# Attention with a mixture of experts on one core: the beginning, the router's order and the passage to the experts, changed together

## The chip, the cores and the metric

The kernel runs on one core of a Trainium2 chip. The metric is the device time of one execution in microseconds (us); several runs give a median, and one more execution is recorded by the hardware profiler. PE is TensorE, DVE is VectorE, ACT is ScalarE, POOL is GpSimd and SP is SyncE, which here only issues DMAs.

## The reference, cut to what matters

The input x has 8 batches of 1024 tokens and 512 features, in float32. The layer is attention with sine and cosine features, then a mixture of 8 experts.

```python
t = arange(S).reshape(1, S, 1, 1); xh = layernorm(x).reshape(B, S, H, dh)       # H 16, dh 32
Q = concat(cos, sin of xh / (1 + |w_q|) + b_q + t * phi_q)      # table of 2048 points
K = concat(cos, sin of xh / (1 + |w_k|) + b_k + t * phi_k)
V = cos + sin of xh / (1 + |w_v|) + b_v
attn = softmax(causal(Q K^T / sqrt(2 * dh))); o = attn V
x = x + cos + sin of o / (1 + |w_out|) + b_out
xn = layernorm(x)
probs = softmax(xn Wr + br); top_p, top_e = top_k(probs, 2)
slot of a token in its expert = its place in order, kept if under 160 for each batch
y = relu(rows W1[e] + b1[e]) W2[e] + b2[e]                      # W1 512x2048, W2 2048x512
x = x + sum over its two experts of top_p * y
```

## The kernel before, in words

All of it is one function. The order of the work on PE, DVE, ACT and SP is the order of the program text; POOL's instructions alone are placed by a scheduler. The text gets its fine order from generators: a piece of work yields at points where other work may be put between, and `some`, `rest` and `with_asides` advance such generators by a step or to their end.

**Beginning** (until the loop). `load_x(0)` (L147) issues eight DMAs of 256 KB on SP for the first batch. ACT's queue issues three row loads (w_v, b_v, b_out, L167), then six for `vec_in`, from which PE and DVE make `vecs`, the columns of constants for q and k. `first_stats` and `layernorm_first` normalise batch 0 on DVE. `make_base(c)` (L443) makes the table t * phi + b for four heads (index c), reduced to one turn: an iota and, for c < 2, the affine step on POOL, the rounding on ACT or DVE, and a 1 MB write to `base_d`, from which later batches read it back. Tables 0 and 1 are made before the loop, 2 and 3 inside of it by `load_base`. Table 1 lies in the buffer of `x_mid` (`room[0]`), as does the scratch for rounding (`room[1]`).

**Attention loop.** It runs over n = 0 to 31, n = 4 b + c: batch b, four heads c. In a step PE makes scores of the heads of n in two pairs (`ps_s`, three buffers of two banks), ACT takes their exponentials (`e`), PE multiplies them with v (`attend`, `av`) and turns the result by token (`turn`). Beside it run, for later steps, `qk_pre` (turning xn, and qk_f by DVE, L508), the sines on ACT, `qk_post` (products on DVE and DMAs into the tiles `qk`), `v_pre` and `v_post`, `layernorm1` of the next batches, and `o_pre`, `o_post` for n - 1, which add the attention's result to `x_mid`.

**Router.** At the first step of a batch (`begin`) the router of the batch before starts: statistics, `rstd`, then four groups of two `rows` (xn on DVE, a DMA to `xn_d`), `features` (PE turns them, DVE copies them to `xT`) and `sums` (logits). Then come the choice of two experts and the places. `scatter` writes for each token its number and gate to a list of slots in DRAM, in 16 indirect DMAs on POOL; `fetch_slots` reads the lists into `meta`. `route_on(slot)` advances the router by a step where the text calls it.

**Passage.** At the last step `experts_begin` opens the experts' buffers, loads the first W1 tiles and runs `gather(0)`: six indirect DMAs on POOL fetch 128 rows of xn each, which PE turns. `experts` runs over 16 chunks (expert e; 768 or 512 of its slots) with layer 1 and layer 2 as seven products in place of eight (`product`; six buffers `ps_p` of one bank). Inside chunk 0 the generator `ending` is advanced once for each product of layer 1: it holds `o_post` and the router of the last batch. `mix_w1` makes sums of weights, on POOL in chunk 0. In `layer2` the results are added to the output by `send`, an accumulating indirect DMA on POOL.

Of the kernel before, what the change touches and what calls it, by code (L numbers as in the profile page):

```python
# [11 lines left out]
F32 = mybir.dt.float32  # L12
# [9 lines left out]
P = 128  # L22
# [51 lines left out]
def preln_attn_moe_kernel(  # L74
# [64 lines left out]
    xnp = to_inputs.pool("xnp", 4, **right)  # L139

# [3 lines left out]
    def token_tiles(dram_rows):  # L144
        return dram_rows.rearrange("(t p) d -> p t d", p=P)

    def load_x(b):  # L147
        halves = []
        for h in range(2):
            xt = xnp.tile([P, 4, D], F32, name="xn")  # L150
            if b == 0:
                for t in range(4):
                    nc.sync.dma_start(xt[:, t, :], token_tiles(x[b])[:, 4 * h + t, :])
            else:
                nc.sync.dma_start(xt, token_tiles(x[b])[:, 4 * h : 4 * h + 4, :])
            halves.append(xt)
        xn_tiles[b] = halves


    load_x(0)  # L160

    rows_in, spare = (
        row2.tile([P, D], F32, name="xn2").rearrange("p (i f) -> p i f", f=P)[:NCH, :n, :]
        for n in (3, 2)
    )
# [56 lines left out]
    first_stats(0, 1)  # L222
# [6 lines left out]
    nc.scalar.dma_start(rows_d.rearrange("i (c f) -> c i f", c=NCH), rows_in)  # L229
# [108 lines left out]
    qkt = to_inputs.pool("qkt", 1, **right)  # L338
# [102 lines left out]
    room = []  # L441

    def make_base(c):  # L443


        if not room:
            t = xmp.tile([P, NTT, D], F32, name="x_mid").rearrange("p (i t) d -> p i (t d)", i=2)
            room.extend(t[:, i, :].rearrange("p (i s) -> p i s", i=2) for i in range(2))
# [3 lines left out]
        nc.gpsimd.iota(  # L452
            p, pattern=[[0, 2], [1, S]], base=0, channel_multiplier=0,
            allow_small_or_imprecise_dtypes=True,
        )
# [28 lines left out]
    def load_base(n):  # L484
        if 1 < n < NCH:
            rest(make_base(n))
            return
# [256 lines left out]
    scatters = []  # L744

    def scatter():
        while scatters:
            b, idx, src = scatters.pop(0)
            nc.gpsimd.indirect_dma_start(  # L749
                out=slot_d[b], out_offset=bass.IndirectOffsetOnAxis(ap=idx, axis=0),  # L750
                in_=src, in_offset=None,
            )

    def router(b):
# [28 lines left out]

        last = b == B - 1

        def features(g):
# [67 lines left out]
        for g in range(NTT // 2):  # L854
            xT = features(g)
            yield
# [91 lines left out]
    def fetch_slots(b):  # L948
# [3 lines left out]
        while s0 < (b + 1) * CAP:  # L952
            s1 = min((s0 // P + 1) * P, (b + 1) * CAP)
            nc.gpsimd.dma_start(
                meta[s0 % P : s0 % P + s1 - s0, :, s0 // P, :],
                rows[s0 - b * CAP : s1 - b * CAP],
            )
# [73 lines left out]
    def gather(i):  # L1031

        e, j0, nh = chunks[i]
        xe = pools["xep"].tile([P, NCH, 2, HALF], F32, name="xe")
        for j in range(2 * nh):
            xg = pools["gp"].tile([P, D], F32, name="xg")
            nc.gpsimd.indirect_dma_start(  # L1037
                out=xg, out_offset=None, in_=xn2_d[i % 2],
                in_offset=bass.IndirectOffsetOnAxis(ap=source[:, e, j0 + j, None], axis=0),
            )  # L1040
            yield None
            dst = xe[:, :, j // nh, j % nh * P : (j % nh + 1) * P]
            if i == 0:
# [6 lines left out]
                )  # L1050
            else:
# [14 lines left out]

    def start(gen, box):
# [6 lines left out]
    def mix_w1(i, q):  # L1074
# [6 lines left out]
        mix = nc.gpsimd.tensor_tensor if i == 0 else TT  # L1081
# [52 lines left out]
    def layer2(i, block, hs, aside):  # L1134
# [29 lines left out]
        def send(r):  # L1164
            nc.gpsimd.indirect_dma_start(  # L1165
# [3 lines left out]
            )  # L1169

# [5 lines left out]
        TT(u2, p1, product(5, 4), ALU.add)  # L1176
        TT(u3, u2, product(6, 5), ALU.add)
        p5 = product(4, 3)
        TT(u2, u2, p5, ALU.add)
        TT(u2, u2, p3, ALU.add)  # L1180
        gated(0, 1, u2)
        send(0)
# [16 lines left out]
    def experts_begin():  # L1199
# [55 lines left out]
    next(base0)  # L1255
    rest_of_loads()
    mask()
    first_stats(1, NTT)
# [6 lines left out]
    next(base1)  # L1265
# [204 lines left out]
```

## Time and profile before

| | |
|---|---|
| Median of three runs | 3331.85 us (3321.11 to 3336.68) |
| Profiled execution | 3330.72 us, its span 3329.0 us |
| PE busy | 3203.4 us, 96% of the span |
| DVE, ACT, POOL busy | 2272.0, 1320.9, 429.5 us |
| PE busy in 0 to 150 us | 91.73 us, granted clock 0.92 |
| PE busy in 150 to 1240 us (attention) | 1061.17 of 1090 us, clock 1.00 |
| PE busy in 1240 to 1480 us (passage) | 216.67 of 240 us, clock 0.94 |
| PE busy in 1480 to 3329 us (experts) | 1833.79 of 1849 us, clock 1.00 |

The page gives the share of the span in which each engine is busy, the span in 40 slices, and the costliest groups of instructions by line. A line is that of kernel.py. A wait is told as "engine, tile, line <- what ended the wait". The timeline shows instructions in order of time: start, duration, engine, line, operation, output and input tiles, and in brackets the idle time before it and its cause. The granted clock is the share of TensorE's full clock that the hardware allowed.

### The profile page before, as it was taken

Reading aid. Unit: us, or ns where it says so; the run is one execution under the profiler, and the core shown is the slowest. Engines: PE = TensorE matmul, PEld = TensorE weight load, DVE = VectorE, ACT = ScalarE, POOL = GpSimd, SP = SyncE. Lnnn points to the kernel's source line nnn. Section 1 sums busy time; section 2 is a strip of 40 time slices with the busy share of each in tenths; the row PEclk is TensorE's granted clock in tenths of the full one; section 3 lists DMA queues with packets and bytes.
Section 4 is the critical chain, followed back from the end, with each engine's and each line's share of the span. In section 5 each row is a group of like instructions: output and inputs, shape, how many; then the busy total and the mean of one; then the engine's idle time right before and its main releaser. Section 6 shows DMA issues by size and latency. Waiting matters only on the chain.

```text
span 3329.0 us, 48774 instructions
## 1 busy us (share of the span) xinstructions
PE 3203.4 (96%) x18942; PEld 2172.0 (65%) x18942; DVE 2272.0 (68%) x4975; ACT 1320.9 (40%) x1617; POOL 429.5 (13%) x397
## 2 busy tenths in 40 slices
PE   3999999999999998899999999999999999999998
PEld 1444444444444444588688688688688688688687
DVE  7887878788787675746746846845845845845854
ACT  5788888878787874201101201201201201201201
POOL 2000202020111103321011011011011011011010
PEclk8999999999999999999999999999999999999999
DMA  4445353545535342422322322322322422322321
GB/s 133 117 121 168 106 165 101 167 134 147 174 106 153 87 143 78 126 39 73 111 38 71 114 42 64 117 39 64 117 45 58 121 42 61 119 46 61 114 39 26
DMA packets 234462, 319.74 MB, mean 96 GB/s; under 512 B 21640, under 2 KB 154488, under 8 KB 222200
## 3 DMA queue, kind: packets, MB, share of 16 engines
q1 hardware_dynamic: 211232, 273.37, 27.8%
q0 software_dynamic: 22912, 43.22, 7.4%
q8 instruction: 150, 2.46, 0.3%
q14 instruction: 80, 0.66, 0.1%
q10 hardware_dynamic: 88, 0.02, 0.0%
HBM read 187.62 MB, written 61.82 MB: 75 GB/s over the span
## 4 chain that ended last, share of the span: by engine, by line
PE 59%; DVE 2%; DMA 1%; issue 0%; ACT 0%; POOL 0%; SPq 0%; POOLq 0%; DVEq 0%; ACTq 0%
PE ps_p L1143 28%; PE ps_p L1098 28%; PE av L701 1%; PE ps_t L1054 1%; PE ps_s L667 1%; DMA out_dram<-y,slots 0%; DMA xg<-xn_d,source 0%; DMA xn_d<-xn 0%; DMA w<-in_L_ffn_W_dram 0%; DVE y L1159 0%; PE ps_s L200 0%; DVE w_t L1009 0%; DVE w L1008 0%; DVE t L1083 0%; DVE u L1185 0%
## 5 line engine op out<-in xcount | busy, mean ns | idle before, releaser
L687 ACT ACTIVATE e<-ps_s 128x1024 f32<-128x1024 f32 (+1 forms) x640 | 567.8, 938 | 212.0 <-PE ps_s L667 130.8
L667 PE MATMUL ps_s<-qk 64*128 64x512 f32 (+3 forms) x3072 | 599.4, 508 | 48.5 <-DVE qk_f L508 20.2
L1143 PE MATMUL ps_p<-w,hid 128*128 128x256 f32 x2560 | 569.6, 380 | 0.0
L1143 PEld LDWEIGHTS ps_p<-w,hid 128*128 128x128 f32 x2560 | 484.6, 190 | 66.3
L701 PE MATMUL av<-e,v 128*64 128x512 f32 (+3 forms) x3072 | 526.6, 492 | 0.0
L1143 PE MATMUL ps_p<-w_t,hid 128*128 128x256 f32 x1920 | 430.3, 379 | 0.6 <-DVE w_t L1009 0.6
L667 PEld LDWEIGHTS ps_s<-qk 64*128 64x128 f32 x3072 | 263.3, 189 | 233.3 <-issue 109.4
L1143 PEld LDWEIGHTS ps_p<-w_t,hid 128*128 128x128 f32 x1920 | 361.8, 190 | 48.7 <-DVE w_t L1009 1.0
L701 PEld LDWEIGHTS av<-e,v 128*64 128x64 f32 x3072 | 201.4, 137 | 285.1 <-issue 269.5
L1098 PE MATMUL ps_p<-xe_s,t 128*128 128x256 f32 (+1 forms) x1024 | 299.3, 435 | 4.3 <-DVE t L1083 3.4
L1098 PE MATMUL ps_p<-xe,w 128*128 128x256 f32 (+1 forms) x1024 | 301.8, 438 | 1.1 <-issue 1.1
L1098 PE MATMUL ps_p<-xe,t 128*128 128x256 f32 (+1 forms) x1024 | 296.8, 433 | 0.0
L749 POOL DMA_INDIRECT slot_d<-token,slot x128 | 161.1, 1259 | 1014.1 <-issue 697.3
L1172 ACT COPY p<-ps_p 128x256 f32<-128x256 f32 x40 | 14.8, 369 | 612.9 <-PE ps_p L1143 612.9
L1098 PEld LDWEIGHTS ps_p<-xe_s,t 128*128 128x128 f32 x1024 | 194.4, 191 | 89.4 <-DVE t L1083 7.9
L1098 PEld LDWEIGHTS ps_p<-xe,w 128*128 128x128 f32 x1024 | 194.8, 192 | 83.9 <-issue 4.9
L1098 PEld LDWEIGHTS ps_p<-xe,t 128*128 128x128 f32 x1024 | 194.4, 190 | 80.9 <-issue 0.4
L1037 POOL DMA_INDIRECT xg<-xn_d,source x80 | 78.1, 976 | 1102.8 <-PE ps_t L1054 1020.9
L1165 POOL DMA_INDIRECT out_dram<-y,slots x80 | 126.3, 1579 | 661.8 <-DVE y L1160 522.4
L1113 ACT ACTIVATE p<-ps_p,b_t 128x256 f32<-128x256 f32 (+1 forms) x128 | 65.4, 511 | 330.7 <-DVE y L1159 169.7
L1117 ACT ACTIVATE hid<-hid 128x256 f32<-128x256 f32 (+1 forms) x128 | 60.1, 470 | 321.7 <-DVE hid L1116 321.7
L1130 ACT ACTIVATE hid<-hid,b_more 128x256 f32<-128x256 f32 (+1 forms) x128 | 71.8, 561 | 271.5 <-DVE hid L1129 271.5
(217 smaller groups left out, 3844.8 us busy)
## 6 DMA issues: line engine op xcount, KB each, us to landing
w<-in_L_ffn_W_dram SPq DMA_DIRECT2D x256, 256.0 KB
w<-in_L_ffn_W_dram SPq DMA_DIRECT2D x64, 512.0 KB
qk<-qk_c SPq DMA_DIRECT2D x124, 256.0 KB
qk<-qk_r SPq DMA_DIRECT2D x124, 256.0 KB
qk_base<-base_d SPq DMA_DIRECT2D x28, 1024.0 KB
xn_d<-xn SPq DMA_DIRECT2D x72, 256.0 KB
x_mid<-in_L_attn_x_dram SPq DMA_DIRECT2D x16, 1024.0 KB
out_dram<-x_mid SPq DMA_DIRECT2D x8, 2048.0 KB
```

What stands on the lines that cost most here:

```text
L667: nc.tensor.matmul(ps[:, a, at : at + w], lhsT=pair[r, 1, kb * P : (kb + 1) * P], rhs=pair[r, 0, q0 : q0 + w], start=at == 0, stop=not own ...
L687: nc.scalar.activation(e, ps[:, :, :n], AF.Exp, scale=UNIT * UNIT / math.sqrt(2 * DH))
L701: nc.tensor.matmul(av[a * 64 : (a + 1) * 64, q0 - 512 * h :], lhsT=vt[:, kb, 2 * pr + a, :], rhs=es[i][:, a, at : at + w], start=kb == 0, ...
L749: nc.gpsimd.indirect_dma_start(out=slot_d[b], out_offset=bass.IndirectOffsetOnAxis(ap=idx, axis=0), in_=src, in_offset=None,)
L1037: nc.gpsimd.indirect_dma_start(out=xg, out_offset=None, in_=xn2_d[i % 2], in_offset=bass.IndirectOffsetOnAxis(ap=source[:, e, j0 + j, None ...
L1054: nc.tensor.transpose(ps[:, c, :], xg[:, c * P : (c + 1) * P], ident)
L1098: nc.tensor.matmul(ps, lhsT=weights[:, k, :], rhs=rows[:, k, :], start=k == 0, stop=k == 1)
L1113: nc.scalar.activation(p1, product(b11, a11), AF.Identity, bias=b1_t[:, e * NHC + q : e * NHC + q + 1])
L1117: nc.scalar.activation(h11, h11, AF.Relu)
L1130: nc.scalar.activation(h12, h12, AF.Relu, bias=more)
L1143: nc.tensor.matmul(ps, lhsT=hs[k][:, part, cols], rhs=ws[k][weight], start=k == 0, stop=k == NHQ - 1,)
L1165: nc.gpsimd.indirect_dma_start(out=out, out_offset=bass.IndirectOffsetOnAxis(ap=meta[:, e, jj[r], 0:1], axis=0), in_=ys[r], in_offset=None ...
```

## The change

At the beginning the six loads of `vec_in` become the first on ACT's queue, and the row loads go to SP behind two tiles of x, spread over 128 partitions. The iotas of tables 0 and 1 come before all that needs `vecs`; two memsets go from POOL to DVE. Table 3 is made inside step 0, in the buffer of table 1, and used there; it is not read back. `layernorm1(1, 1)` is no longer called at step 0 (it was called there and at step 2). `load_mid(0)` goes to the end of step 1.

In the router, `v_post` of the next step and the next two `rows` go behind qk_f at `begin`, with one more yield in a group, and the calls of `route_on` in a batch's second step (c = 1) are placed anew. The scatters of a batch are declared free of each other, and `fetch_slots` waits for all of them.

In the passage the rows of slots for chunk 0 are found two steps before the loop's end, the first two gathers go into `xn2` buffers there, and the next two run ahead. `experts` reuses PSUM tile by tile. The last router has more products between its stages (6 behind "tiles", 5 behind "places"), the last two sums of W1 in chunk 0 are on DVE, one W1 load and `find_rows(1)` and `gather(1)` come earlier, and the sends of chunk 0 are pinned behind the gathers. In `layer2`, for all chunks, the product p5 comes before product(6, 5) and `send(0)` follows it.

```diff
@@ -146,0 +148,6 @@
+    rows_in, spare = (
+        row2.tile([P, D], F32, name="xn2").rearrange("p (i f) -> p i f", f=NCH)[:, :n, :]
+        for n in (3, 2)
+    )
@@ -153,0 +161,8 @@
+                    if (h, t) == (0, 1):
+                        for i, v in enumerate((w_v, b_v)):
+                            nc.sync.dma_start(
+                                rows_in[:, i, :], v.rearrange("h (a f) -> (h a) f", f=NCH)
+                            )
+                        nc.sync.dma_start(
+                            rows_in[:, 2, :], b_out.rearrange("(p f) -> p f", f=NCH)
+                        )
@@ -160,9 +174,0 @@
-    load_x(0)
-
...
-    for i, v in enumerate((w_v, b_v)):
-        nc.scalar.dma_start(rows_in[:, i, :], v.rearrange("(c h) d -> c (h d)", h=HPC))
-    nc.scalar.dma_start(rows_in[:, 2, :], b_out.rearrange("(c f) -> c f", c=NCH))
@@ -173,0 +180 @@
+    load_x(0)
@@ -175,0 +183,8 @@
+    base_first = qkt.tile([P, 2, S], F32, name="qk_base")
+    t = xmp.tile([P, NTT, D], F32, name="x_mid").rearrange("p (i t) d -> p i (t d)", i=2)
+    room = [t[:, i, :].rearrange("p (i s) -> p i s", i=2) for i in range(2)]
+    for t in (base_first, room[0]):
+        nc.gpsimd.iota(
+            t, pattern=[[0, 2], [1, S]], base=0, channel_multiplier=0,
+            allow_small_or_imprecise_dtypes=True,
+        )
@@ -222 +237 @@
-    first_stats(0, 1)
+    first_stats(0, 2)
@@ -229 +244 @@
-    nc.scalar.dma_start(rows_d.rearrange("i (c f) -> c i f", c=NCH), rows_in)
+    nc.scalar.dma_start(rows_d.rearrange("i (p f) -> p i f", f=NCH), rows_in)
@@ -266 +281 @@
-    nc.gpsimd.memset(zero, 0.0)
+    nc.vector.memset(zero, 0.0)
@@ -268 +283 @@
-    nc.gpsimd.memset(empty, 0)
+    nc.vector.memset(empty, 0)
@@ -446,4 +458,3 @@
...
-        p = qkt.tile([P, 2, S], F32, name="qk_base") if c != 1 else room[0]
+        p = (base_first, room[0])[c] if c < 2 else (
+            qkt.tile([P, 2, S], F32, name="qk_base") if c == 2 else room[0]
+        )
@@ -450,0 +462,5 @@
+        if c > 1:
+            nc.gpsimd.iota(
+                p, pattern=[[0, 2], [1, S]], base=0, channel_multiplier=0,
+                allow_small_or_imprecise_dtypes=True,
+            )
@@ -452,4 +467,0 @@
-        nc.gpsimd.iota(
-            p, pattern=[[0, 2], [1, S]], base=0, channel_multiplier=0,
-            allow_small_or_imprecise_dtypes=True,
-        )
@@ -485 +497 @@
-        if 1 < n < NCH:
+        if n == 2:
@@ -486,0 +499 @@
+        if n < NCH:
@@ -744,0 +758 @@
+    scattered = {b: [] for b in range(B)}
@@ -749 +764 @@
-            nc.gpsimd.indirect_dma_start(
+            ins = nc.gpsimd.indirect_dma_start(
@@ -752 +767,4 @@
-            )
+            ).ins
+            for other in scattered[b]:
+                tc.declare_no_dep(ins, other, reason="rows of their own")
+            scattered[b].append(ins)
@@ -765,0 +784,3 @@
+        last = b == B - 1
+        if last:
+            yield
@@ -766,0 +788,2 @@
+        if last:
+            yield
@@ -806,4 +826,0 @@
-            if g + 1 < NTT // 2:
-                ahead[:] = [rows(2 * g + 2), rows(2 * g + 3)]
-                if not last and 2 * g + 4 == NTT:
-                    store()
@@ -811,0 +829,5 @@
+        def next_rows(g):
+            ahead[:] = [rows(2 * g + 2), rows(2 * g + 3)]
+            if not last and 2 * g + 4 == NTT:
+                store()
+
@@ -855,0 +878,4 @@
+            if g + 1 < NTT // 2:
+                if not last:
+                    yield
+                next_rows(g)
@@ -957 +983,9 @@
-            )
+            ).ins
+            for other in scattered[b]:
+                tc.add_manual_dep(
...
@@ -1034,4 +1068,2 @@
-        xe = pools["xep"].tile([P, NCH, 2, HALF], F32, name="xe")
-        for j in range(2 * nh):
-            xg = pools["gp"].tile([P, D], F32, name="xg")
-            nc.gpsimd.indirect_dma_start(
+        def fetch(xg, j):
+            ins = nc.gpsimd.indirect_dma_start(
@@ -1040,0 +1073,11 @@
+            if i in (1, 2):
+                tc.keep_in_program_order(ins)
+            return xg
+
+        def fetch_next(j):
+            return fetch(pools["gp"].tile([P, D], F32, name="xg"), j)
+
+        there = []
+        if i == 0:
+
+            there = [fetch(row2.tile([P, D], F32, name="xn2"), j) for j in range(2)]
@@ -1041,0 +1085,8 @@
+            there += [fetch_next(j) for j in (2, 3)]
+        xe = pools["xep"].tile([P, NCH, 2, HALF], F32, name="xe")
+        for j in range(2 * nh):
+            if len(there) == j:
+                there.append(fetch_next(j))
+            if j or i:
+                yield None
+            xg = there[j]
@@ -1050,0 +1102,2 @@
+                if 1 < j and j + 2 < 2 * nh:
+                    there.append(fetch_next(j + 2))
@@ -1066,0 +1120,5 @@
+    def behind(count, gen):
+        for _ in range(count):
+            yield
+        yield from gen
+
@@ -1081 +1139,2 @@
-        mix = nc.gpsimd.tensor_tensor if i == 0 else TT
+
+        mix = nc.gpsimd.tensor_tensor if i == 0 and q < 6 else TT
@@ -1165 +1224 @@
-            nc.gpsimd.indirect_dma_start(
+            ins = nc.gpsimd.indirect_dma_start(
@@ -1169,0 +1229,2 @@
+            if i == 0:
+                tc.keep_in_program_order(ins)
@@ -1177 +1237,0 @@
-        TT(u3, u2, product(6, 5), ALU.add)
@@ -1179,3 +1239,3 @@
-        TT(u2, u2, p5, ALU.add)
-        TT(u2, u2, p3, ALU.add)
-        gated(0, 1, u2)
+        TT(p1, u2, p5, ALU.add)
+        TT(p1, p1, p3, ALU.add)
+        gated(0, 1, p1)
@@ -1182,0 +1243 @@
+        TT(u3, u2, product(6, 5), ALU.add)
@@ -1203 +1263,0 @@
-        find_rows(0)
@@ -1206 +1266 @@
-        yield from start(gather(0), first_parts)
+        yield from start(first_gather, first_parts)
@@ -1211,2 +1271,2 @@
-        pools["ps_tr"] = to_end.pool("ps_tr", 2, space=PSUM)
-        pools["ps_p"] = to_end.pool("ps_p", 6, space=PSUM)
+        pools["ps_tr"] = to_end.pool("ps_tr", 2, space=PSUM, reuse_waits="tile")
+        pools["ps_p"] = to_end.pool("ps_p", 6, space=PSUM, reuse_waits="tile")
@@ -1219 +1279,2 @@
-                load_ahead(i * NHQ + q + AHEAD)
+                if i or q != NHQ - AHEAD - 1:
+                    load_ahead(i * NHQ + q + AHEAD)
@@ -1230,0 +1292 @@
+                    load_ahead(NHQ - 1)
@@ -1235,0 +1298,2 @@
+            if i == 0:
+                find_rows(1)
@@ -1237,0 +1302,3 @@
+            if i == 0:
+
+                aside = behind(2, aside)
@@ -1239,3 +1306 @@
-                if i == 0 and block == 1:
-                    find_rows(1)
-                layer2(i, block, hs, aside if i or block else iter(()))
+                layer2(i, block, hs, aside)
@@ -1255,0 +1321 @@
+    next(base1)
@@ -1258 +1324 @@
-    first_stats(1, NTT)
+    first_stats(2, NTT)
@@ -1265 +1330,0 @@
-    next(base1)
@@ -1273,0 +1339 @@
+    first_gather = gather(0)
@@ -1280,0 +1347,3 @@
+        if n == NCK - 2:
+            find_rows(0)
+            next(first_gather)
@@ -1295 +1364 @@
-        elif c == 0 and b + 1 < B:
+        elif c == 0 and 0 < b < B - 1:
@@ -1320,0 +1390,3 @@
+            if begin:
+                v_post(n, v_st)
+                next(route)
@@ -1322,0 +1395,2 @@
+            if n == 0:
+                rest(make_base(3))
@@ -1327,2 +1401,2 @@
-        route_on(1)
-        route_on(1)
+        for _ in range(3):
+            route_on(1)
@@ -1339,2 +1412,0 @@
-        if n == 1:
-            load_mid(0)
@@ -1344,0 +1417 @@
+        route_on(1)
@@ -1386,0 +1460 @@
+            route_on(1)
@@ -1391 +1464,0 @@
-        route_on(1)
@@ -1396 +1469 @@
-        if c == 1 and b > 0:
+        if c == 1:
@@ -1400 +1473 @@
-        if more:
+        if more and not begin:
@@ -1427,2 +1500 @@
-        rest(o_post(NCK - 1, o_st))
-        for _ in range(3):
+        for _ in o_post(NCK - 1, o_st):
@@ -1429,0 +1502 @@
+        yield
@@ -1432 +1505 @@
-            for _ in range(5 if name == "tiles" else 1):
+            for _ in range({"tiles": 6, "places": 5}.get(name, 1)):
```

More of the change, by code (lines that the diff above doesn't have):

```diff
@@ L139, in preln_attn_moe_kernel @@
     xnp = to_inputs.pool("xnp", 4, **right)
+    qkt = to_inputs.pool("qkt", 1, **right)
     xn_tiles = {}
@@ L157, in load_x @@
         xn_tiles[b] = halves
-    load_x(0)
-    rows_in, spare = (
-        row2.tile([P, D], F32, name="xn2").rearrange("p (i f) -> p i f", f=P)[:NCH, :n, :]
-        for n in (3, 2)
-    )
-    for i, v in enumerate((w_v, b_v)):
-        nc.scalar.dma_start(rows_in[:, i, :], v.rearrange("(c h) d -> c (h d)", h=HPC))
-    nc.scalar.dma_start(rows_in[:, 2, :], b_out.rearrange("(c f) -> c f", c=NCH))
     vec_in = own.tile([6 * NCH, P], F32, name="vec_in")
@@ L337, in preln_attn_moe_kernel @@
     qkp = to_pairs.pool("qkp", 3, **left)
-    qkt = to_inputs.pool("qkt", 1, **right)
     ps_av = to_pairs.pool("ps_av", 2, space=PSUM)
@@ L439, in preln_attn_moe_kernel @@
     bases = {}
-    room = []
     def make_base(c):
-        if not room:
-            t = xmp.tile([P, NTT, D], F32, name="x_mid").rearrange("p (i t) d -> p i (t d)", i=2)
-            room.extend(t[:, i, :].rearrange("p (i s) -> p i s", i=2) for i in range(2))
-        p = qkt.tile([P, 2, S], F32, name="qk_base") if c != 1 else room[0]
+        p = (base_first, room[0])[c] if c < 2 else (
+            qkt.tile([P, 2, S], F32, name="qk_base") if c == 2 else room[0]
+        )
         r = room[1]
+        if c > 1:
[3 more added lines that the diff above has]
+            )
         affine = nc.gpsimd.tensor_scalar if c < 2 else nc.vector.tensor_scalar
-        nc.gpsimd.iota(
-            p, pattern=[[0, 2], [1, S]], base=0, channel_multiplier=0,
-            allow_small_or_imprecise_dtypes=True,
-        )
         for i in range(2):
@@ L782, in rows @@
             return xn
-        last = b == B - 1
         def features(g):
@@ L953, in fetch_slots @@
             s1 = min((s0 // P + 1) * P, (b + 1) * CAP)
-            nc.gpsimd.dma_start(
+            ins = nc.gpsimd.dma_start(
                 meta[s0 % P : s0 % P + s1 - s0, :, s0 // P, :],
                 rows[s0 - b * CAP : s1 - b * CAP],
-            )
+            ).ins
+            for other in scattered[b]:
+                tc.add_manual_dep(
+                    ins, other.name,
+                    mybir.DependencyInfo(
+                        mybir.DependencyClass.Sync, mybir.DependencyReason.DATA
+                    ),
+                    reason="rows of all scatters",
+                )
             s0 = s1
@@ L1176, in layer2 @@
         TT(u2, p1, product(5, 4), ALU.add)
-        TT(u3, u2, product(6, 5), ALU.add)
-        p5 = product(4, 3)
-        TT(u2, u2, p5, ALU.add)
-        TT(u2, u2, p3, ALU.add)
-        gated(0, 1, u2)
-        send(0)
+        p5 = product(4, 3)
+        TT(p1, u2, p5, ALU.add)
+        TT(p1, p1, p3, ALU.add)
+        gated(0, 1, p1)
+        send(0)
+        TT(u3, u2, product(6, 5), ALU.add)
         TT(ys[1][:, DC:], u3, p5, ALU.add)
```

## The prediction

> **What bounds the kernel now.** The page comes first, for the bound and its holes: its slices, busy tenths of PE and PE's granted clock.
>
> ```profile
> PE   3999999999999998899999999999999999999998
> PEclk8999999999999999999999999999999999999999
> ```
>
> TensorE (PE) is the bound: busy 3203.4 us of the 3329.0 us span. A gain must come from the 126 us in which it is not busy, or from time at a reduced clock. I asked next for PE's waits over the whole span (columns: us in total, times, longest).
>
> ```profile
> PE ps_s L667 <- DVE qk_f L508: 20.2, 7, 7.7
> PE ps_s L200 <- DVE xn L419: 16.4, 1, 16.4
> PE ps_s L667 <- DMA qk<-qk_r: 12.4, 1, 12.4
> PE ps_s L667 <- ACT e L687: 10.3, 7, 5.1
> ...
> PE ps_s L838 <- DVE xT L802: 6.6, 8, 0.8
> PE ps_t L1054 <- DMA xg<-xn_d,source: 4.2, 1, 4.2
> PE ps_s L667 <- DVE xT L802: 3.9, 7, 0.7
> PE ps_t L821 <- DVE prior L904: 3.5, 1, 3.5
> ```
>
> Asked again by stretch, they make four places. **Beginning** (0 to 150 us): 58 us, the 16.4, 12.4 and 10.1 (for vec_in) before the first scores at 42.06 us, then 7.7 for qk_f, 5.3 and 2.9 for exponentials, 2.6 for o_p. **Routers**: 3.1 to 4.6 us in each of seven passes, 23 us in the rows of qk_f (20.2 less 7.7), xT at L838 and xT at L667. **Passage** (1240 to 1480 us, attention to experts): 22.6 us. **Experts**: none from 1500 us on, PE busy 50.00 of 50 us in nearly every stretch, so what changes there in steady state is worth nothing. A few timeline lines carry the rest (start us, us).
>
> ```profile
> 20.74 1.85 DVE L348 TENSOR_SCALAR rstd<-rstd_v 128x8 int32<-128x8 int32 x1
> ...
> 20.70 1.86 POOL L452 IOTA x_mid<- 128x2048 f32 x1
> ...
> 1311.05 4.51 PE L1098 MATMUL ps_p<-xe,w 128*128 128x384 f32 x8 [1.13 <-issue]
> 1315.39 2.74 PE L1098 MATMUL ps_p<-xe_s,t 128*128 128x384 f32 x8
> ...
> 1290.29 0.97 POOL L749 DMA_INDIRECT slot_d<-token,slot  x1 [1.46 <-DMA slot_d<-token,slot]
> ...
> 3321.37 1.55 POOL L1165 DMA_INDIRECT out_dram<-y,slots  x1 [4.03 <-DMA out_dram<-y,slots]
> ```
>
> [...] an 8-column tensor_scalar took 1.85 us beside the iota above, 0.17 us at 244.68 with POOL idle. [...] Eight 384-column matmuls took 4.51 us after the turn into the experts and 2.74 us next; [...] The scatters agree: 0.97 us of POOL, then 1.46 us of waiting for the one before.
>
> **The change part by part.** The sum is made against the profiled execution, 3330.72 us (span 3329.0 and 1.7 around it); that is 1.1 below the median 3331.85 of the runs.
>
> *Beginning, to the first scores.* vec_in's six loads lead ScalarE's queue: three issues less ahead (0.80 to 2.02 us), so 1.2 us earlier. The three row loads go behind two x tiles on SP and are now 128 pieces of 16 bytes each, a form the trace does not show: between no later than now and 3 us late; their DVE chain stands ahead of the copy of vecs, so lateness eats the 1.2. Of the statistics six instead of seven stand behind vecs: -0.8. The two 1.86 us iotas run before vecs is there, and the two memsets moved to DVE cost 0.4. The rstd chain took 5.6 us (20.54 to 26.12), beside an iota and two POOL tensor_scalars; with POOL idle the same chain took 2.3 us (244.47 to 246.7). With small POOL work beside it I take 2.7: -3. The base on ScalarE must be ready too: POOL 4.8 us after vecs, ScalarE 2.3 more, ahead of rstd. Sum -1.2 - 0.8 - 3 + 0.4 = -4.6; bounds -7 and -1. From the first normalised tile (26.20) to the first scores (42.06) nothing changes. SP's zero fills wait a little longer for the memsets, but SP was idle from 23.4 to 30.4: nothing.
>
> *Beginning, n = 0 and 1.* layernorm1(1, 1) at n = 0 goes: it was done again at c = 2. DVE no longer waits 6.8 us for batch one's x, and qk_f comes 8.4 us earlier, so the 7.7 wait goes. But make_base(3) stands next in DVE's order, ahead of t_r. It works in the buffer of base one, so its iota on POOL waits until SP's 1 MB write of that base has landed. That write was issued at 47.48 behind 2 MB of x; DMA was busy until 57.75. Then, in the old clock: landed 58.5, iota 60.4, DVE's 6.3 us (the 100.38 to 106.76 block) 66.7, t_r 67.4, v_p's square 68.5. Behind that square stand the exponentials that PE waits for; they began at 67.25. So +1.2: the 5.1 us wait grows by what the 7.7 us one gave. Bounds: -4 (write landed by 54), +3. At n = 1 DVE loses that 6.3 us block, which made t_r late (110.63) and PE wait 2.92 us; after it 384-column scores ran at 1.98 us for eight against 1.09, so -3.9 with the ramp; bounds -4.5 and -1. make_base(2) and its 2.6 us wait stay. x_mid's 2 MB load moves from mid n = 1 to its end, as in the other batches: nothing, covered by a whole half-pass. **Beginning: -4.6 + 1.2 - 3.9 = -7.3; -15 to +1.**
>
> *Routers, seven passes.* DVE had v (1.22) at 247.68 and xn rows (0.99) at 250.67 ahead of qk_f; both go behind. av_sb must await av until 248.2, so xT starts about 0.5 sooner and qk_f ends 1.3 us sooner than 254.3: of the 1.6 us wait 0.3 stays. xT at L667 goes (0.5). Later in the pass xT goes ahead of qk_f: L838's 0.8 goes, and qk_f ends 1.28 later, where PE has scores and av to do. Sum 2.6 times 7 is 18; I take 14, because qk_r (and ScalarE's squares behind it, which began 1.9 us after it) now waits for 2.2 us of moved work. Bounds: -21, and +8 if that is exposed. The x_n rows' eight DMAs on SP move with them; SP is idle there.
>
> *Passage.* The first two gathers run a pass earlier into xn2, the next two ahead: waits of 2.54 and 2.3 us, and 1.6 of slow matmuls: -5.5, a reserve of 0.9 kept. They stand on POOL ahead of batch 6's scatters (2 us later, needed only in the experts). PSUM reuse by tile at 1311: 1.13 of wait and 1.8 of slow clock; half, -1.5. Router of batch 7 inside chunk 0: 1.7 + 1.9 + 2.4 for xn and xT and 3.4 of slow matmuls; more products lie before the transposes (6 for 5, and DVE's work spread), but xT's copy still has one product to hide in: half, -4.5. "places" gets 5 products, 6.5 us, for 3.5 + 0.7 of waits: -4.2, and 2 of ramp, less 1.2 for what DVE's layer-1 work now stands ahead: -5. The last scatters: 16 at 2.4 us or more, 1378 to 1430; side by side about 1.0 each, so slots, find_rows and gather(1) are ready before PE needs them: 4.2 and about 1 of ramp, -5. Queue order pinned on POOL and the 8 DVE subtractions (some 4 us) that leave POOL: covered by PE at 50 of 50. **Passage: -21.5, taken -20; -30 to -8.**
>
> *Tail.* p5 before product(6, 5) lets send(0) go one product (3.45 us) sooner; send(1) now waits for its landing, 4.03 us. Then DVE's last gating (3318.5) and 0.3 of issue bind, 3318.8 for 3321.15: **-2.3; -3 to -1.**
>
> **Sum:** -7.3 - 14 - 20 - 2.3 = -43.6; 3330.7 - 43.6 = 3287.
>
> **Rivals.**
> A (forecast, 0.70): as above, 3265 to 3306.
> B, waits take the place of waits (0.17): routers give 4, passage 8, beginning 0, tail 2: 3317. For it: in the experts' router DVE and ScalarE alternate within one product, and reordering only moves who is late. Against: 2.4 us of each scatter is waiting, not work, and the tail is a plain chain.
> C, everything gives (0.07): beginning 15, routers 18, passage 28, tail 3: 3267 and below.
> D, slower (0.06): in each router pass the squares of qk_f come late behind v, rows and xT, the next qk is late and PE waits at L667. The other three places give 30, so D decides from 4.3 us a pass on; at 6 it gives 3331 - 30 + 42 = 3343. Against: 1.9 us of slack before the squares, and ScalarE idles 5 us at 282 to 287.
> That the change does not do what it says is a form of B: the scatters would keep 2.4 us of spacing.
>
> **How the numbers follow.** 0.5% (about what a measurement of this kernel can tell from no change) is 17 us, so faster means below 3315: all of A and C and nearly half of B, 0.85; same 0.09, most of B's rest; slower 0.06. The likeliest is A's 3287. The range reaches into B and C: 3264 to 3314.
>
> **What would show it.** First scores near 37 us; PE's 7.7 us wait for qk_f gone but one of 10 us or more for an exponential at n = 0; no wait over 1 us for qk_f in the passes; scatters about 1 us apart; no wait for prior or for xg; POOL's last send 2 us after the last matmul. Wrong if the scatters stay 2.4 us apart, or if PE's waits in 1240 to 1480 us still sum to over 15 us.

## The result, and the profile after

The changed kernel takes 3361.97 us (median; 3357.28 to 3372.11) against 3331.39 us for the kernel before (one run more than in the table above): 1.011 of it, 95% interval 1.0088 to 1.0131. It is slower by 31 us, where 44 us less were forecast. Its profiled execution took 3362.41 us, span 3360.7.

The slices of the page after, PE busy and PE's granted clock in tenths, hardly show where:

```profile
PE   4999999999999998999999999999999999999998
PEclk8999999999999998999999999999999999999999
```

The first slice gained (4 for 3). The next fourteen read 9 as before, because a tenth of an 84 us slice hides 8 us; only the clock's digit falls once, from 9 to 8, in the slice of batch 6's scatters. The totals do show it: the changed kernel's PE is busy for 1040.80 us of 150 to 1240 us, where it was 1061.17. The waits tell more. The profile calls a releaser that it cannot name "remote". The changed kernel has such waits, of ACT and DVE (us in total, times, longest):

```profile
ACT e L700 <- remote: 28.7, 10, 14.5
...
DVE qk_f L521 <- remote: 13.4, 4, 3.4
...
DVE rec L749 <- remote: 10.4, 1, 10.4
```

The kernel before has none. PE's waits over the whole span in the changed kernel (us in total, times, longest):

```profile
PE ps_s L680 <- ACT e L700: 20.6, 9, 9.6
PE ps_s L215 <- DVE xn L433: 13.6, 1, 13.6
PE ps_s L680 <- DMA qk<-qk_r: 12.4, 1, 12.4
PE ps_s L680 <- DVE qk_f L521: 9.1, 9, 4.2
PE ps_s L680 <- issue: 9.0, 6, 2.5
PE ps_s L215 <- issue: 6.3, 5, 1.3
...
PE ps_s L680 <- DVE o_p L751: 5.1, 1, 5.1
PE ps_s L680 <- DVE rec L749: 4.3, 3, 1.6
```

(L680 and L700 after are L667 and L687 before: scores and exponentials.) The row of qk_f has fallen from 20.2, its longest from 7.7, as forecast. New are 15.3 us of waits for "issue", for which the profile shows no releaser (1.1 before), and 9.4 us of waits of L680 for o_p and rec, which had no row before. The scatters of a batch run in bursts of 16. A stretch with such a burst, by engine, first before (columns: PE, PEld, DVE, ACT, POOL busy, PE's clock, DMA share, GB/s):

```profile
500.00:540.00 40.00, 39.95 (x316) 19.37 (x314) 33.95 (x68) 35.96 (x35) 13.49 (x9) 1.00 0.33 80
```

and after:

```profile
500.00:540.00 40.00, 34.29 (x236) 15.62 (x232) 27.99 (x58) 27.07 (x28) 21.69 (x19) 0.91 0.35 80
```

POOL has issued this burst in 23 us in place of 62, and PE, DVE and ACT all lost 6 to 9 us in the same 40. The timeline of the changed kernel in batch 6 shows how:

```profile
1322.98 0.66 PE L215 MATMUL ps_s<-ident,av_sb 64*128 64x64 f32 x16
...
1326.21 2.01 PE L680 MATMUL ps_s<-qk 64*128 64x512 f32 x4 [0.85 <-ACT e L700]
1326.89 0.95 POOL L764 DMA_INDIRECT slot_d<-token,slot  x1 [0.30 <-issue]
1328.15 0.96 POOL L764 DMA_INDIRECT slot_d<-token,slot  x1 [0.30 <-issue]
...
1332.15 0.26 DVE L749 RECIPROCAL rec<-ps_s 128x16 f32<-128x16 f32 x1 [10.43 <-remote]
1332.44 0.69 DVE L751 TENSOR_TENSOR o_p<-ps_s,rec 128x512 f32<-128x512 f32 x1
1333.28 2.08 PE L680 MATMUL ps_s<-qk 64*128 64x512 f32 x4 [5.06 <-DVE o_p L751]
...
1340.18 1.59 POOL L980 DMA_DIRECT2D slots<-slot_d  x2 [2.22 <-DMA slot_d<-token,slot]
1340.66 0.60 ACT L700 ACTIVATE e<-ps_s 128x512 f32<-128x512 f32 x1 [14.51 <-remote]
```

The reciprocal needs only the 16 transposes, which ended at 1323.64. It starts 8.5 us later. ACT stands still for 14.51 us, until the last scatter has landed. From 1328.2 to 1332.1 nothing runs but POOL's scatters, 1.26 us apart (0.96 and 0.30). The work is done; the **signal** that it is done comes late. A signal is here a semaphore event in the trace, on which another engine's wait ends. These can be counted. From a burst's start to 4 us after its last scatter has started, the kernel before has 240 to 256 recorded landing signals of 256 (16 scatters by 16 signals), the changed one 39 to 89. (Even up to the next transfer, which waits for all scatters, the changed kernel has no more than 40 to 95: most landings left no record of their own.) PE's signals come late too. In the kernel before half of them come within 0.02 us of a matmul's end, the latest 0.08 after. In batch 6 of the changed kernel the one for the transposes comes at 1332.12, 8.5 us after their end, and those for two groups of scores, ended at 1325.35 and 1328.22, come at 1340.58 and 1340.64: 15.2 and 12.4 us. That DVE's and ACT's signals are late is not shown: those recorded come within 0.02 us, and after each of PE's waits of over 0.8 us in the bursts PE starts within 0.2 us of the end of a DVE or ACT instruction. But 62 of DVE's 4372 and 27 of ACT's 1473 have no record; in the kernel before it is one, of ACT's.

### The profile page after: what moved, and what is told of

Read it like the earlier page. It is cut to its first block, busy times and chain, and to the rows that moved or that the text cites. A ratio compares the mean times of both kernels' runs of the same rounds, so it can differ in the third digit from the quotient of the medians.

```text
span 3360.7 us, 48765 instructions
## 1 busy us (share of the span) xinstructions
PE 3221.9 (96%) x18942; PEld 2173.8 (65%) x18942; DVE 2252.0 (67%) x4961; ACT 1323.6 (39%) x1617; POOL 417.0 (12%) x387
## 4 chain that ended last, share of the span: by engine, by line
PE 83%; DVE 9%; issue 2%; ACT 2%; DMA 1%; another core or an unknown queue 1%; POOL 0%; SPq 0%; POOLq 0%; DVEq 0%; ACTq 0%
PE ps_p L1202 28%; PE ps_p L1157 25%; PE av L714 14%; PE ps_s L680 12%; ACT e L700 2%; PE ps_s L215 1%; PE ps_s L694 1%; DVE qk_f L521 1%; PE ps_t L1107 1%; DVE qk_r L450 1%; DVE v L450 0%; DVE xT L823 0%; DMA xg<-xn_d,source 0%; ACT hid L1189 0%
## 5 line engine op out<-in xcount | busy, mean ns | idle before, releaser
L700 ACT ACTIVATE e<-ps_s 128x1024 f32<-128x1024 f32 (+1 forms) x640 | 570.2, 938 | 274.4 <-PE ps_s L680 140.7
L680 PE MATMUL ps_s<-qk 64*128 64x512 f32 (+3 forms) x3072 | 612.2, 514 | 66.2 <-ACT e L700 20.6
L714 PE MATMUL av<-e,v 128*64 128x512 f32 (+3 forms) x3072 | 537.2, 500 | 3.5 <-ACT e L700 3.5
L680 PEld LDWEIGHTS ps_s<-qk 64*128 64x128 f32 x3072 | 266.6, 191 | 262.2 <-issue 135.4
L1202 PEld LDWEIGHTS ps_p<-w_t,hid 128*128 128x128 f32 x1920 | 361.9, 190 | 50.4 <-DVE w_t L1043 2.8
```

Source lines behind the costliest of these rows:

```text
L680: nc.tensor.matmul(ps[:, a, at : at + w], lhsT=pair[r, 1, kb * P : (kb + 1) * P], rhs=pair[r, 0, q0 : q0 + w], start=at == 0, stop=not own ...
L700: nc.scalar.activation(e, ps[:, :, :n], AF.Exp, scale=UNIT * UNIT / math.sqrt(2 * DH))
L714: nc.tensor.matmul(av[a * 64 : (a + 1) * 64, q0 - 512 * h :], lhsT=vt[:, kb, 2 * pr + a, :], rhs=es[i][:, a, at : at + w], start=kb == 0, ...
L1202: nc.tensor.matmul(ps, lhsT=hs[k][:, part, cols], rhs=ws[k][weight], start=k == 0, stop=k == NHQ - 1,)
```

## The experiments

Theory **H**: the unchained scatters (none waits for the one before) hold back signals, and the rest of the change gains as forecast. Rival **R**: the router's new order costs the time. Kernels told of together ran on the same chip, beside the kernel before. The chips are called A to F; that of the first comparison is not known. The time in the table is a median; ratios are to the kernel before on that chip. "Last av" is the start of the last matmul of attention with v; "experts" is from there to the end of the last matmul, "tail" from that to the span's end, all from the profiled execution. Each execution here has a recorded span and clock. None was made without recording, so whether recording the signals is part of their load stays untested.

| kernel | chip | time, us | ratio (95%) | last av | experts | tail |
|---|---|---|---|---|---|---|
| before | - | 3331.4 | 1 | 1308.2 | 2009.0 | 11.8 |
| changed | - | 3362.0 | 1.0088-1.0131 | 1354.4 | 1997.1 | 9.2 |
| e1 one by one | A | 3332.3 | 1.0016-1.0041 | 1288.0 | 2030.1 | 9.1 |
| e2 before, side by side | A | 3329.4 | 1.0008-1.0026 | 1308.2 | 2010.5 | 11.7 |
| e3 "spaced" | A | 3301.2 | 0.9919-0.9952 | 1293.6 | 1998.7 | 9.1 |
| e4 "half spaced" | A | 3300.7 | 0.9918-0.9951 | 1293.2 | 1998.5 | 9.2 |
| e5 changed again | B | 3362.6 | 1.0087-1.0131 | 1352.2 | 1999.6 | 9.2 |
| e6 pad alone | B | 3363.0 | 1.0082-1.0129 | 1354.0 | 1996.8 | 9.2 |
| e7 last two side by side | B | 3314.3 | 0.9950-0.9976 | 1302.1 | 1996.3 | 9.2 |
| e8 changed, third | C | 3390.1 | 1.0162-1.0207 | 1392.7 | 1997.7 | 9.2 |
| e9 "spaced" again | C | 3400.3 | 1.0195-1.0234 | 1391.4 | 1998.4 | 9.3 |
| e10 before, side by side | C | 3417.5 | 1.0255-1.0304 | 1393.4 | 2011.3 | 11.7 |
| e11 changed | D | 3391.6 | 1.0155-1.0210 | 1382.0 | 1997.8 | 9.2 |
| e12 wide rows | D | 3375.1 | 1.0111-1.0163 | 1363.1 | 1996.0 | 9.2 |
| e13 four fills between | D | 3326.5 | 0.9979-0.9993 | 1291.0 | 2022.3 | 9.6 |
| e14 two fills between | D | 3313.5 | 0.9932-0.9966 | 1289.3 | 2011.5 | 9.1 |
| e15 fills but last | E | 3302.1 | 0.9919-0.9947 | 1291.2 | 1999.9 | 9.1 |
| e16 chain but last | E | 3305.7 | 0.9930-0.9957 | 1288.3 | 2008.3 | 9.2 |
| e17 gather bursts | E | 3305.5 | 0.9930-0.9960 | 1289.4 | 2005.7 | 8.5 |
| e18 the same again | F | 3303.2 | 0.9919-0.9946 | 1287.6 | 2005.3 | 8.4 |

**Undoing one part, doing it alone (A).** e1 takes the scatters' freedom away, e2 gives it to the kernel before.

```diff
 # e1: scatter() and fetch_slots() as before; e2: these lines added to before
-            for other in scattered[b]:
-                tc.declare_no_dep(ins, other, reason="rows of their own")
```

> The changed kernel with its slot_d scatters waiting for one another again, as before. Theory H (in the changed kernel, 16 scatters 1.26 us apart hold back the signals between the other engines for up to 12 us, some 5 us a batch): the time falls from 3362 by 35 to 60 us, to 3300-3325, below the 3331 of the kernel before; the engines' signals land within 0.1 us again. Rival R (the new order of the router's parts is what costs, and the scatters only show it): the time stays within 10 us of the changed kernel, 3352-3372.

> The kernel before with nothing changed but that its slot_d scatters no longer wait for one another. H: slower than before by 35 to 60 us (3366-3390), with scatters 1.26 us apart and late signals in every batch. R: no slower than before, 3320-3335, since the router's order is the old one.

Both missed. e1 is 30 us below the changed kernel (whose chip is not known), but at 1.0029 of before, not under it. Its attention gained the full 20.2 us (1308.2 to 1288.0) and its experts gave back 21.1. PE's waits of e1 from 1240 to 1500 us name it:

```profile
PE ps_p L1191 <- DVE w_t L1032: 24.7, 6, 22.3
PE ps_p L1146 <- POOL t L1131: 6.7, 1, 6.7
PE ps_s L215 <- DMA xg<-xn_d,source: 3.3, 1, 3.3
```

and DVE's timeline in e1 what stands ahead of that w_t:

```profile
1416.46 0.18 DVE L1049 TENSOR_SCALAR source<-slots 128x32 int32<-128x32 int32 x1 [26.46 <-DMA slots<-slot_d]
1416.56 0.43 DVE L1030 TENSOR_TENSOR w_t<-w 128x256 f32<-128x256 f32 x1
```

The change puts `find_rows(1)` earlier, ahead of the sums of W2 on DVE. It needs the last batch's slots. With scatters 2.4 us and more apart these come at 1416, DVE waits 26.46 us and PE 22.26. So the close scatters are worth 31 us to the new passage (2030.1 against 1998.7 in e3), not the 5 of my sum. e2 is the surprise: scatters 1.26 us apart, the same last av as before, and 0.17% lost in all. For H it had to lose 35 to 60 us.

**Room between the scatters (A).**

```diff
             b, idx, src = scatters.pop(0)
+            for _ in range(4 if scattered[b] else 0):    # e4: 2
+                nc.gpsimd.memset(pad, 0.0)
```

> The changed kernel, scatters still without waits for one another, but with four small fills of a scratch tile (128x256, some 0.3 us each) on GpSimd ahead of each, so that they start about 2.5 us apart. If it is the rate of the scatters that delays the signals: as one by one, within 8 us of it, 3300-3330. If it is that they are not ordered (several in flight, or the waits on them): as the changed kernel, 3350-3370.

> The same with two fills, scatters about 1.9 us apart. If a backlog builds up above a rate that lies near the 2.0 us one scatter takes to land: little is lost, 3305-3335. If the loss goes with how closely they are packed: between the changed kernel and the spaced one, 3330-3350.

The question was not put: POOL's scheduler moved all fills to the beginning (first scores at 38.9 instead of 34.5 us), and the scatters stayed 1.26 us apart. Yet both took 3301 us, with 244 to 256 landing signals a burst. (The 2.0 us in the second expectation is a little low: in the kernel before a scatter landed after 2.1 us at the least, 3.0 in the median.) Close scatters, nothing held back: either these builds differed from the changed one, or the chip did.

**Build or chip (B, C).** e5, e8 and e11 are the changed kernel, e9 is e3, e10 is e2. e6 has e3's tile and one fill on DVE. e7 chains all batches but the last two.

```diff
 # e6
+    pad = own.tile([P, 256], F32, name="pad"); nc.vector.memset(pad, 0.0)
 # e7, likewise in fetch_slots
-            for other in scattered[b]:
+            for other in scattered[b] if b > B - 3 else ():
```

> The changed kernel once more, unaltered, since its scatters 1.26 us apart held the signals back and those of the three other kernels with unchained scatters (which started just as closely, the fills having been moved to the beginning) did not. If the holding back belongs to this build (where its tiles and scatter lists lie): 3355-3372 again, some 40-90 landing signals recorded of 256 in a burst. If it was the chip or the occasion of that run: about 3296 (the spaced kernel's 3301 less the 4.4 us by which the fills put off the first scores), range 3290-3306, and 240 or more signals of 256.

> The changed kernel with the scratch tile of the spaced kernels (128x256, 1 KB a partition, which moves what lies above it) and a single fill of it on VectorE; no fills on GpSimd. If the place of tiles decides: no stalls, 3290-3302, while the unaltered kernel is at 3355-3372. If it is the fills' instructions on GpSimd: as the changed kernel, 3355-3372. If occasion or chip: the same as the unaltered kernel of this call.

> The changed kernel with the scatters of batches 0 to 5 one by one and those of the last two batches side by side. One by one the passage was 199 us (last attention value to the 320th product of layer two), side by side 168, and the attention steps need no closeness. If nothing is held back in the last two batches: 3290-3302. If held back there as in the changed kernel (some 17 us in batch 6's burst): 3308-3322.

B looked like the build: e5 and e6 lose in every batch (46 to 94 of 256 signals). C settled it:

> The changed kernel unaltered, for the third time, now on the same chip as the spaced kernel and the kernel before with unchained scatters: so far the kernels with unchained scatters that kept their signals ran on one chip and those that lost them on another. If it is the build: 3357-3372 with 40-90 landing signals of 256 in a burst, while the spaced kernel beside it stays at 3301. If it is the chip: all three fall alike, either this one near 3296 with 240 or more signals, or all three held back.

> The spaced kernel unaltered (its fills run at the beginning, its scatters start 1.26 us apart). Build: 3301 again, 240-256 signals of 256 a burst. Chip: as the unaltered changed kernel plus 4 us: 3301 if that is near 3296, 3360-3375 if that is near 3362.

> The kernel before with only its scatters unchained, unaltered. Build: 3325-3335 again (1.000 to 1.003 of before). Chip, and the chip is one that holds signals back: slower than before by 40-75 us, 3365-3400. Chip, and it is one that does not: 3325-3335.

All three are held back there, with 31 to 92 of 256 signals; e10 loses 90 us, more than the 40 to 75 forecast. e2 and e10 are one kernel: 3329.4 on A, 3417.5 on C. So are e3 and e9: 3301.2 and 3400.3. It goes with the chip (or the occasion; the runs cannot tell these two apart), not with the build. **R falls** too: e10 loses with the router's old order, and e3 and e9 differ by 98 us at the last av in one and the same order. The rows of all matmuls with v (duration min/median/max in ns, first and last start), for e3:

```profile
L714 PE MATMUL av<-e,v x3072: 272/592/1113, 69.9 to 1293.6; 128*64 128x512 f32 x192
```

and for e9, the same kernel on chip C:

```profile
L714 PE MATMUL av<-e,v x3072: 272/592/1114, 69.9 to 1391.4; 128*64 128x512 f32 x192
```

The matmuls themselves last as long; they start later. e7 adds a point: on B the last batch's close burst was held back (42 of 256 signals) and cost the experts nothing, 1996.3; the burst of batch 6 cost attention 14 us (1302.1 for 1288.0).

**Rate, or being unchained, or short rows (D).** In e13 and e14 the fills, and the scatters with them, are pinned to the order of the text. In e12 the rows have 64 bytes (and four small tiles one buffer each, to make room).

```diff
 # e13; e14 with 2
+            for _ in range(4 if scattered[b] else 0):
+                tc.keep_in_program_order(nc.gpsimd.memset(pad, 0.0))
 # e12: slot_d, token and empty 16 wide, fetch_slots reads the first 2
-        token = tok.tile([P, NTT, TOPK, 2], I32, name="token")
+        token = tok.tile([P, NTT, TOPK, 16], I32, name="token", bufs=1)
+        nc.vector.memset(token[:, :, :, 2:], 0)
```

> The changed kernel unaltered, as the reference for the chip that this call gets: 3355-3395 with 30-95 of 256 landing signals recorded a burst on a chip that holds signals back, about 3296 with 240 or more on one that does not.

> The changed kernel with 64-byte rows in slot_d and token in place of 8-byte ones (one more fill of 128x224 a batch on VectorE), at the same 1.26 us. If it is the short writes that back up [...]: nothing is held back, 3292-3302 on any chip. If it is the number of scatters or of their signals: as the unaltered kernel, within 12 us.

> The changed kernel, scatters unchained, four fills of 0.35 us pinned ahead of each scatter after the first, so some 2.7 us apart. If the rate decides: no late signals, attention as one by one (last attention value near 1288), and a passage between the side-by-side 168 and the one-by-one 199 us: 3300-3335. If it is their being unchained that decides: 3350-3395 on a chip that holds signals back.

> The same with two fills, some 2.0 us apart. If the rate decides with a limit between 1.3 and 2.0 us: no late signals, 3295-3320. If the limit lies above 2.0: part of the unaltered kernel's loss, 3320-3370.

The rate decides, as far as these four runs can tell. e14's timeline in batch 6, beside full PE work:

```profile
1283.37 0.96 POOL L767 DMA_INDIRECT slot_d<-token,slot  x1 [0.16 <-issue]
...
1283.86 5.81 PE L714 MATMUL av<-e,v 128*64 128x512 f32 x32
1284.33 0.70 POOL L766 MEMSET pad<- 128x256 f32 x2
1285.19 0.96 POOL L767 DMA_INDIRECT slot_d<-token,slot  x1 [0.16 <-issue]
```

At 1.82 us apart, still unchained, attention ends at 1289.3; on the same chip at 1.26 us it ends at 1382.0. e13, some 2.6 to 3.1 us apart, ends it at 1291.0. No run pins the scatters without fills on this chip, but the pinning did not move them: the first burst starts at 337.8 us in e11 and at 337.9 in e14. In 500 to 540 us PE of e14 is busy for

```profile
500.00:540.00 40.00, 38.68 (x296) 18.46 (x294) 32.25 (x58) 33.69 (x35) 23.40 (x37) 1.00 0.39 87
```

against e11, at a clock of 0.87:

```profile
500.00:540.00 40.00, 29.72 (x214) 13.80 (x210) 23.92 (x50) 22.55 (x25) 19.74 (x19) 0.87 0.40 80
```

Some landing signals are missing even at 1.82 (156 to 215 of 256 recorded), but little waits for them: the last av comes 1.3 us after that of e1, whose scatters are chained. Wide rows do not help: 24 to 76 of 256 signals, 3375.1. That is 17 us under e11, more than the 12 I allowed, so rows may matter a little; they are not the cause. What the fills cost is the slower last burst: experts take 2011.5 and 2022.3 us, for 1998 with a close one.

**Which arrangement keeps the gain (E, F).** e15 has two fills in batches 0 to 6, e16 the chain there; in both the last batch's scatters are close. e17 adds to e16 16 gathers (8-byte rows of x, unused) in each of batches 1 to 5.

```diff
 # e15, on e14
-            for _ in range(2 if scattered[b] else 0):
+            for _ in range(2 if scattered[b] and b < B - 1 else 0):
 # e16, on the changed kernel, likewise in fetch_slots
-            for other in scattered[b]:
+            for other in scattered[b] if b == B - 1 else ():
```

> The changed kernel, scatters unchained, two pinned fills ahead of each in batches 0 to 6 (some 1.8 us apart), none in the last batch. If a close burst in the last batch costs little, since it lies beside the experts' first products: last attention value near 1289, passage 166-170, 3294-3302 on any chip. If it holds up the passage too: 3305-3325 on a chip that holds signals back.

> The changed kernel with the scatters of batches 0 to 6 waiting for one another and those of the last batch unchained and close. As the one with fills, 3292-3305, if batch 6's slower burst (31-40 us against 29) is over before the last batch's; with a later passage by up to 10 us, 3300-3312, if it is not.

> As chain-but-last, with a burst of 16 added indirect gathers (8-byte rows of the input into a scratch tile, results unused) after the scatters of batches 1 to 5, about 1.26 us apart. If only scattered writes to DRAM hold the signals back: within 8 us of chain-but-last and all landing signals of these gathers recorded. If any burst of indirect transfers does: slower by 7-14 us a batch where the chip holds signals back, 35-70 us in all (the last batch's scatters show whether it does).

> The kernel with chained scatters but for the last batch, and bursts of 16 added gathers, unaltered. If the last batch's burst of scatters has 90 or fewer of 256 landing signals (a chip that holds signals back): with gathers harmless, the attention steps of batches 1 to 5 stay at 36-37 and 44.5 us and the time at 3298-3312; with gathers as bad as scatters, one step in each of five batches is 5-14 us longer, 3325-3370; in both the passage (last attention value to the 320th product of layer two) tells what the last batch's burst costs, 160-182 us. On a chip that holds nothing back: 3300-3310 again, and both questions stay open.

All beat the kernel before: e15 by 0.67% (0.53 to 0.81), e16 by 0.56%. But E and F let the last batch's close burst pass (240 or more of 256 signals), so two questions stay open: whether bursts of gathers hold signals back (e17 and e18 lost nothing), and the time of e15 and e16 where signals are held. e14 is the best one measured on such a chip, 3313.5. e16 shows where the chain still costs time. Its experts take 8.4 us more than e15's; 6.5 of them are one wait of PE for a sum of weights `t`, which POOL begins only after the chained scatters of batch 6. e15 has no such wait. That e15 would do as well where signals are held as on E is an inference from e14 (attention) and e7 (experts), not a measurement.

## Why the prediction was wrong

**The step that failed** is the pricing of the scatters side by side. The prediction gave them -5, in the passage alone: "side by side about 1.0 each, so slots, find_rows and gather(1) are ready". Beside attention, where the bursts of seven batches run, they stood in the sum at nothing, without a reason given. That part costs, in the recorded execution, 66 us: last av at 1354.4 against 1288.0 in e1, where only this is undone. (e1 ran on A, but with chained scatters the last av is 1288.3, 1289.4 and 1287.6 on E and F too, in e16 to e18. On one and the same chip, D, e11 is 93 us behind e14.) The terms close on the spans: -20.2 (attention without it) + 66.4 - 11.9 (experts) - 2.6 (tail) = 31.7 = 3360.7 - 3329.0. I costed a change of rate as a gain of latency only. The rate itself was read too roughly as well: the scatters came 1.26 us apart, not 1.0, and of the 2.4 us that I called waiting, against rival B, my own line has 1.46 as waiting and 0.97 as work. No rival held a loss by disturbance; "slower" was given 0.06, for another cause.

**Beginning and routers: right together, shares off.** -7.3 and -14 make -21.3; e1 measured -20.2, e16 -19.9. First scores came at 34.5, not 37; but that number carries less than I thought, since the kernel before with only its scatters freed had them at 37.0 and 39.0 instead of 42.1, and on A still reached its last av at 1308.2. The 7.7 us wait for qk_f has become one of 4.0 (e16), so it is not gone, and the new wait for an exponential is there, 9.6 us (10.9 in e16) for "10 us or more". Routers gave less. PE's waits from 150 to 1240 us in e16:

```profile
PE ps_s L860 <- DVE xT L823: 5.5, 7, 0.8
PE ps_s L680 <- DVE prob L867: 4.0, 7, 0.6
PE ps_s L680 <- DVE qk_f L521: 3.9, 7, 0.6
PE ps_s L843 <- DVE lg L865: 3.4, 7, 0.6
```

No wait for qk_f is over 0.6 us, as forecast, and xT at L667 is gone. But xT at L838 before, which I took out, kept 5.5 us of 6.6 (L860 after), and the rows of prob and lg sum to 7.4 us, for 0.5 before: they are what is late next. With two rows of exponentials the waits sum to 18.7 us against 26.6 before, 8 us for the 14 forecast. That leaves some 12 to the beginning, by subtraction; its waits in 0 to 150 us fell by 7.7 us (58.1 to 50.4), and the clock there is 0.94 in e1, for 0.92 before. The chain of rstd, 5.6 us before beside POOL instructions of up to 1.9 us, took 2.4 in the changed kernel (16.24 to 18.59) beside ones of up to 0.3. The forecast's "ramp" and "slow clock" are PE's slower matmuls after a wait: in the kernel before eight 384-column scores took 1.98 us behind the wait of 2.92, and 1.09 at 1301.09; the clock was 0.76 from 113 to 120 us and 0.81 from 1312 to 1320. Whether the wait lowers the clock no run tests; what the forecast took for it was my estimate.

**Passage: half.** -20 forecast; with close scatters experts take 1996 to 2000 us for 2009.0, so -9 to -13. The longest wait for `prior` fell from 3.5 to 0.7. The first gathers gave almost nothing, where I took 5.5 us out: the waits at them, ahead of the last av, were 4.8 us before (2.5 put down to `t`, 2.3 to xg) and are 4.5 in e3 (1.8 and 2.7). The wait at `gather(1)` fell from 4.2 to 1.7. And `find_rows(1)` moved ahead of the sums of W2, which I costed at nothing, has its cover in the close scatters alone: without them it is the 22.26 us wait of e1.

**Tail: right.** -2.3 forecast, -2.6 measured (11.8 to 9.2), the last send 1.6 us after the last matmul. From the changed kernel's timeline:

```profile
3352.47 0.35 DVE L1219 TENSOR_SCALAR y<-y,slots 128x256 f32<-128x256 f32 x1
3353.09 1.56 POOL L1224 DMA_INDIRECT out_dram<-y,slots  x1 [4.90 <-DVE y L1219]
```

**The rivals.** B's form did not come (the scatters are 1.26 us apart). D's mechanism did not come either: PE's waits in the passes of e16, listed above, have no next qk that is late. It named the right sign for a wrong reason. On a chip that holds nothing back the changed kernel itself was not run; e3 with 4.4 us less at the beginning gives an estimate of 3297, inside the range and 10 above the forecast. But the kernel before took 3323 on that chip, not 3331, so the gain would be 26 us, not 44.

## What to carry to other kernels

Here unchaining small DMAs raised their rate (one scatter in 1.26 us, for 2.4 and more), and on chips B, C and D the rate was a load on the whole core (in the changed kernel the last av came 64 to 105 us later than in e1): price such a change as a cost, at the place where most of the DMAs run, and not only as a gain where the last one is waited for. Free the order only where the latency is needed (here the last batch), and leave space elsewhere. When all engines idle together and the releaser is unknown, look at when the work that should release them ended; here the gaps of 10.4 us on DVE and 14.5 on ACT were late signals. A repeat on another chip belongs before any story about the build.

## What the runs showed of the hardware

- During 16 indirect scatters of 128 rows, 1.26 us apart, the landing signals recorded fell to 39 to 89 of 256 (changed kernel), and PE's signals to DVE and ACT came up to 15.2 us late (batch 6), the first late ones for matmuls that ended some 5 us into the burst in batches 0 to 6. In e11 PE was busy for 29.72 of 40 us beside such a burst; at 1.82 us apart on the same chip (e14) for 38.68, and the last av came 1.3 us after that of e1.
- It happened on chips B, C and D, and on that of the first comparison, and not on A, with the same kernels (e2 and e10, e3 and e9). Its cost differed: the time over the kernel before was 36 us on B, 60 to 90 on C and D.
- On the chips that held signals back, recorded landing signals of such bursts were 24 to 95 of 256. In batch 6 of the changed kernel the packets left all the same: 16 of 64 bytes and 16 of 4 bytes a scatter, all within 1.8 us of its start, as in 11 of the 16 scatters there in the kernel before. So it is not the packets that are late; where the delay of the signals arises, no run shows.
- Fills on POOL written between DMAs were moved ahead, to the beginning of the kernel (e3, e4: first scores at 38.9 us for 34.5), unless their order was pinned (e13, e14).
